# The attentions' output bias, added on GpSimd tile by tile instead of in a run of four

## The chip, the cores and the metric

The kernel runs on one core of one Trainium2 chip. The core has five engines that run side by side, each through its own queue of instructions in a fixed order: TensorE (PE in the profile, with its weight loads as PEld), VectorE (DVE), ScalarE (ACT), GpSimd (POOL) and SyncE (SP, which issues most transfers). They wait for one another by semaphores. The metric is the time of one execution on the device, in microseconds (us).

## The reference, cut to what matters

The input `x` is 2 x 2048 rows of 512 values in f32. Two layers follow each other, each made of a gated cross attention over 128 context rows and a gated feed-forward part:

```python
x = x + tanh(g_xattn[0]) * L0_xattn(layernorm(x), ctx)   # 16 heads of 32
x = x + tanh(g_ffn[0])   * L0_ffn(layernorm(x))          # runs on 256 rows a batch, chosen by a router
x = x + tanh(g_xattn[1]) * L1_xattn(layernorm(x), ctx)   # 16 heads of 64
x = x + tanh(g_ffn[1])   * L1_ffn(layernorm(x))          # 8-bit rows, ternary weights, a conv of 3 taps

def xattn(x, ctx):
    q, k, v = ...                      # projections of x and of the context, by heads
    out = softmax(q @ k.T * scale) @ v
    return out @ Wo + bo
```

The change is about `bo`, the output bias of the two attentions, and about the residual `x` to which the attention's output is added.

## The kernel before, in words

Rows are worked in eight blocks of 512 rows (`BLK`), four tiles of 128 rows each (`TB` = 4). One function, `cross_attention`, serves both attentions. It is unrolled in Python. Its main loop counts units: one unit is one head of one block, so 16 units a block, and a block's later steps are carried out units behind its earlier ones:

- `scores` (L276, PE) and `probabilities` for unit U: the maximum (L119, DVE), the exponentials (L122, ACT), the reciprocal of their sum (L130, DVE), and the multiplication by it (L131, on POOL, 128 x 512 elements).
- `transposed` (L294, PE, copied out by L295) for unit U - 2, and `values` (L302, PE, copied out by L310) for four units together.
- `front` of the next block in unit 10: layer norm with the power `rsqrt` on POOL (L90), the normalisation on DVE (L104), transposes (L113).
- `queries` (L253, PE) of the next four heads.
- `back`, the output projection of the block before. It is a generator of which each unit takes one step, and each step is half a tile: four (first attention) or eight (second) matmuls L320 into a PSUM tile `pp`, a `yield` after the first half and one after the tile. At a tile's end DVE computes `x = pp * gate + x` (L329) and `pp` is free again. PSUM tiles `pp`, `pq` (of `queries`), and those of the feed-forward's matmuls share two buffers in the first attention and three in the second.

The weights' loader multiplies the bias row, spread over all 128 partitions, by the gate once (`load_rest`, L174), so that `back` needs only `x + bo`, on POOL (L316), before L329.

`residual()` gives the four tiles of the residual. In the first attention they lie in SBUF already; in the second they are loaded again from memory.

Beside the first attention runs the router of the first feed-forward, taken step by step by `beside`: statistics (L806, L807), a dot product (L810), and the ranking of rows by comparisons on DVE (L862, L906). Beside the second attention runs the first half of the second feed-forward, by `beside4`: matmuls L1159, then on DVE the scaling (L1169) and two taps of the convolution (L1175), on ACT the middle tap (L1171), and on POOL two small copies that carry the two last columns from block to block (L1168, L1170); later the maxima (L1208 to L1213) and the rounding to integers (L1258, L1264). The second half (L1388) comes last.

A scheduler decides in which order each engine's instructions stand. `keep_in_program_order` pins an instruction behind what has been written before it for the same engine.

Of the kernel before, what the change touches and what calls it, by code (L numbers as in the profile page):

```python
# [22 lines left out]
TB = BLK // P  # L23
# [20 lines left out]
def flamingo_kernel(ctx: ExitStack, tc: tile.TileContext, a: dict, out: bass.AP):  # L44
# [170 lines left out]
    def cross_attention(  # L215
# [96 lines left out]
        def back(n, residual, OT):  # L312

            tiles = residual()
            for t in tiles:
                tc.keep_in_program_order(nc.gpsimd.tensor_tensor(t, t, W.bo, ALU.add))  # L316
            for i, t in enumerate(tiles):
                pp = ps_mm.tile([P, D], F32, name="pp", tag="mm")
                for e in range(nE):
                    nc.tensor.matmul(  # L320
                        pp,
                        OT[e][:, ts(i, P)],
                        W.wo[:, e, :],
                        start=(e == 0),
                        stop=(e == nE - 1),
                    )
                    if e == nE // 2 - 1:
                        yield
                nc.vector.scalar_tensor_tensor(t, pp, W.g, t, ALU.mult, ALU.add)  # L329
                if i == TB - 1:  # L330
                    after_block(n, tiles)
                yield
# [10 lines left out]
        for U in range(N * H + 12):  # L343
            n, u = divmod(U, H)
            if n < N:
                grp, t = divmod(u, 4)
# [18 lines left out]
            if 0 <= V < N * H and V % 4 == 3:  # L365
                n, grp = divmod(V // 4, 4)
                if grp == 0:
                    OT[n] = []
                values(n // NBLK, [AT.pop(i) for i in range(V - 3, V + 1)], OT[n], grp)
                if grp == 3:  # L370
                    out_of = back(n, residual.pop(n), OT.pop(n))
                    if n == N - 1:
                        after_units()
# [1056 lines left out]
    for g in range(LAST + 1):  # L1430
# [5 lines left out]
        for i in range(TB):  # L1436
            t, r, p = ahead.pop(0)
# [78 lines left out]
```

## Time and profile before

| | |
|---|---|
| median of 3 runs | 1788.83 us (1788.56 to 1795.08) |
| the profiled execution | 1791.24 us, of it 1789.2 in the span of the profile |
| PE busy | 1647.3 us, 92% of the span |
| DVE busy | 1250.1 us, 70% |
| ACT busy | 1101.7 us, 62% |
| POOL busy | 536.0 us, 30% |
| bias adds, L316 on POOL | 64 instructions, 1258 ns at the least, 1294 in the middle, 1917 at the most |
| first and last start of L316 | 83.5 us and 1576.1 us |
| first attention and its surroundings, 0 to 560 us | PE busy 498.8, DVE 379.6, POOL 217.1 |
| second attention, 775 to 1620 us | PE busy 805.4, DVE 656.3, POOL 282.1 |
| granted clock of PE | 0.966 of full speed |

In a row of the profile "x64" is the number of instructions, and a line number is the line of the kernel as it was before. In the view of one line the three durations are the shortest, the middle and the longest. In a timeline row the first number is the start and the second the length, both in us from the span's start; neighbouring instructions of one kind are told as one row, with their number. In square brackets stands how long the engine had been idle and what ended the wait. "Excess" in this text is what an instruction takes beyond the time that the same kind with the same shape takes when nothing is in its way.

### The profile page before, as it was taken

The numbers are of one execution on the slowest core, as the hardware profiler recorded it, in microseconds if no ns is written. First come the engines' busy times: TensorE is split into PE (matmuls) and PEld (weight loads), VectorE is DVE, ScalarE is ACT, GpSimd is POOL, SyncE is SP. The second block draws the span as 40 slices with busy tenths as digits, with TensorE's granted clock in tenths as the row PEclk, the third lists the DMA queues.
The fourth block names the chain that finished last, engine by engine and source line by source line (L and its number), as shares of the span: only waits on it lengthen the run. The fifth ranks groups of instructions, "written<-read, shape, count | busy, mean of one in ns | idle before, by whom it ended". The sixth has DMA issues, their size and how long they took to land.

```text
span 1789.2 us, 25277 instructions
## 1 busy us (share of the span) xinstructions
PE 1647.3 (92%) x8122; PEld 864.8 (48%) x8122; DVE 1250.1 (70%) x2544; ACT 1101.7 (62%) x3170; POOL 536.0 (30%) x671
## 2 busy tenths in 40 slices
PE   6999889899999889999999999999999999889968
PEld 3544444455555665755444544445454544434423
DVE  4566878865767443344378789897998789686956
ACT  2876566456553233345367778787787778744555
POOL 2534443342440011033134242432424224231100
PEclk9999999999999999999999999999999999899979
DMA  6011011121007861630012333233242233157374
GB/s 215 7 66 55 35 60 66 59 65 54 25 36 250 287 190 64 190 83 25 19 53 95 127 122 117 91 130 110 94 167 76 87 105 130 62 210 249 123 233 173
DMA packets 119828, 196.99 MB, mean 110 GB/s; under 512 B 12900, under 2 KB 50532, under 8 KB 115984
## 3 DMA queue, kind: packets, MB, share of 16 engines
q1 hardware_dynamic: 117872, 192.23, 31.5%
q0 software_dynamic: 960, 2.10, 0.6%
q8 instruction: 64, 1.05, 0.2%
q10 hardware_dynamic: 864, 1.05, 0.2%
q14 instruction: 68, 0.56, 0.1%
HBM read 120.89 MB, written 74.45 MB: 109 GB/s over the span
## 4 chain that ended last, share of the span: by engine, by line
PE 29%; DVE 15%; DMA 5%; ACT 4%; issue 2%; POOL 1%; SPq 1%; DVEq 0%; POOLq 0%; ACTq 0%
PE pq L253 8%; PE pp L320 8%; DVE h L1175 4%; PE po L302 3%; PE ph L1159 3%; PE sc L276 3%; PE po L1388 2%; PE tp L294 2%; DMA x<-h_d 1%; DVE u L1169 1%; DVE AT L295 1%; DVE nmx L119 1%; DMA hq<-hq_d 1%; DVE hf L1258 1%; DMA h_d<-h 1%
## 5 line engine op out<-in xcount | busy, mean ns | idle before, releaser
L122 ACT ACTIVATE A<-sc,nmx 128x128 f32<-128x128 f32 x1024 | 363.8, 385 | 131.5 <-DVE nmx L119 121.7
L131 POOL TENSOR_TENSOR A<-A,rden 128x512 f32<-128x512 f32 x256 | 275.9, 1079 | 506.7 <-DVE rden L130 410.8
L320 PE MATMUL pp<-L_wo,OT 128*128 128x512 f32 x768 | 366.8, 609 | 18.0 <-DVE x L329 11.9
L253 PE MATMUL pq<-xnT,L_wq 128*128 128x512 f32 x768 | 345.7, 598 | 12.2 <-DVE x L329 12.2
L122 ACT ACTIVATION_READ_ACCUMULATOR A<-sc,nmx 128x1 f32 x1024 | 229.7, 224 | 0.0
L253 PEld LDWEIGHTS pq<-xnT,L_wq 128*128 128x128 f32 x768 | 142.8, 191 | 172.1 <-issue 151.3
L119 DVE TENSOR_REDUCE nmx<-sc 128x4 f32<-128x512 f32 x256 | 168.6, 678 | 71.8 <-PE sc L276 71.6
L320 PEld LDWEIGHTS pp<-L_wo,OT 128*128 128x128 f32 x768 | 136.5, 193 | 164.4 <-issue 133.2
L1175 DVE SCALAR_TENSOR_TENSOR h<-u,cw,h 128x512 f32<-128x512 f32 x256 | 205.0, 834 | 6.0 <-ACT h L1171 5.5
L294 PE MATMUL tp<-ident,A 128*128 128x128 f32 x1024 | 164.4, 284 | 18.7 <-POOL A L131 13.2
L294 PEld LDWEIGHTS tp<-ident,A 128*128 128x128 f32 x1024 | 118.4, 143 | 87.6 <-issue 41.9
L295 DVE COPY AT<-tp 128x512 f32<-128x512 f32 x192 | 129.8, 678 | 43.5 <-PE tp L294 42.8
L276 PEld LDWEIGHTS sc<-L_kT,qT 32*128 32x128 f32 (+1 forms) x2048 | 110.6, 192 | 71.0 <-issue 58.5
L1388 PE MATMUL po<-w2q,hq 128*128 128x512 bf16 x512 | 122.2, 394 | 20.0 <-DVE hq L1370 9.0
L276 PE MATMUL sc<-L_kT,qT 32*128 32x128 f32 (+1 forms) x2048 | 137.0, 293 | 3.8 <-ACT A L122 3.2
L1171 ACT ACTIVATE h<-u,cb,cw 128x512 f32<-128x512 f32 x128 | 99.1, 808 | 64.7 <-DVE u L1169 53.6
L302 PE MATMUL po<-AT,L_v 128*32 128x512 f32 (+1 forms) x512 | 119.3, 657 | 11.7 <-DVE AT L295 11.1
L1159 PE MATMUL ph<-xiT,w1q 128*128 128x512 bf16 x512 | 124.3, 379 | 1.9 <-DVE u L1169 1.5
L1169 DVE TENSOR_TENSOR u<-ph,inv_b 128x512 f32<-128x512 f32 x128 | 84.9, 682 | 31.4 <-PE ph L1159 27.3
L130 DVE RECIPROCAL rden<-den 128x4 f32<-128x4 f32 x256 | 43.3, 169 | 80.0 <-ACT A L122 72.8
L1168 POOL COPY u<-carry 128x2 f32<-128x2 f32 x128 | 48.7, 382 | 167.3 <-DVE h L1175 141.3
L1170 POOL COPY carry<-u 128x2 f32<-128x2 f32 x128 | 49.8, 394 | 150.9 <-DVE u L1169 149.1
(238 smaller groups left out, 2362.6 us busy)
## 6 DMA issues: line engine op xcount, KB each, us to landing
h_d<-h SPq DMA_DIRECT2D x28, 1024.0 KB, 4.1
x_d<-x SPq DMA_DIRECT2D x64, 256.0 KB, 3.1
hf<-h_d SPq DMA_DIRECT2D x64, 256.0 KB, 3.4
x<-x_d SPq DMA_DIRECT2D x61, 256.0 KB, 4.7
x<-h_d SPq DMA_DIRECT2D x48, 256.0 KB, 5.5
x_d<-xo SPq DMA_DIRECT2D x32, 256.0 KB, 2.1
xf<-x_d SPq DMA_DIRECT2D x32, 256.0 KB, 3.6
hq_d<-hi SPq DMA_DIRECT2D x64, 128.0 KB, 1.8
```

The source lines that it names most:

```text
L119: nc.vector.tensor_reduce(nmx, sc, AX.X, ALU.max, negate=True)
L122: nc.scalar.activation(out_tile[:, h, :], sc[:, h, :], AF.Exp, bias=nmx[:, h : h + 1], accum_out=den[:, h : h + 1],)
L131: nc.gpsimd.tensor_tensor(out_tile, out_tile, rden.unsqueeze(2).to_broadcast([P, n, width]), ALU.mult,)
L253: nc.tensor.matmul(pq, W.wq[:, d, ts(e, P)], xnT[:, d, :], start=(d == 0), stop=(d == DC - 1),)
L276: nc.tensor.matmul(sc[h][:, t, :], qT[e % cpg][r, ts(t, P)], W.kT[r, b, e, :], start=True, stop=True,)
L294: nc.tensor.transpose(tp[:, t, :], A[:, t, :], ident)
L295: copy(AT, tp.rearrange("p t n -> p (t n)"))
L302: nc.tensor.matmul(po[h * dh : (h + 1) * dh, :], W.v[:, b, ts(hd, dh)], AT[c * hpc + h], start=True, stop=True,)
L320: nc.tensor.matmul(pp, OT[e][:, ts(i, P)], W.wo[:, e, :], start=(e == 0), stop=(e == nE - 1),)
L1159: nc.tensor.matmul(ph, w1q[:, d, ts(c, P)], xiT[g][:, d, :], start=(d == 0), stop=(d == DC - 1),)
L1175: nc.vector.scalar_tensor_tensor(z, u[:, ds(k, BLK)], cw[:, c, k : k + 1], z, ALU.mult, ALU.add)
L1388: nc.tensor.matmul(po, rows(c), w2q[:, c, :], start=(c == 0), stop=(c == HC - 1))
```

## The change

The four additions of `back` stood in a loop ahead of the first tile's matmuls, so POOL carried them out in a row. They become a function, `add_bias(i)`. It is called for tile 0 at the start, and for tile i + 1 after the `yield` in the middle of tile i. It still pins the addition behind what has been written before it for POOL. The number of additions, their operands and their results stay as they were.

```diff
         def back(n, residual, OT):
 
             tiles = residual()
-            for t in tiles:
+
+            def add_bias(i):
+
+                t = tiles[i]
                 tc.keep_in_program_order(nc.gpsimd.tensor_tensor(t, t, W.bo, ALU.add))
+
+            add_bias(0)
             for i, t in enumerate(tiles):
                 pp = ps_mm.tile([P, D], F32, name="pp", tag="mm")
                 for e in range(nE):
...
                     if e == nE // 2 - 1:
                         yield
+                        if i + 1 < TB:
+                            add_bias(i + 1)
                 nc.vector.scalar_tensor_tensor(t, pp, W.g, t, ALU.mult, ALU.add)
                 if i == TB - 1:
                     after_block(n, tiles)
```

## The prediction

> **What bounds the kernel now.** I read first the page: the profiled execution took 1791.24 us, 2.0 us of it outside the span. Then the line views of the bias add and of what shares time with it, then the timeline around each of the sixteen runs of adds, and last who waits for the step that takes the biased tile.
>
> ```profile
> span 1789.2 us, 25277 instructions
> ...
> PE 1647.3 (92%) x8122; PEld 864.8 (48%) x8122; DVE 1250.1 (70%) x2544; ACT 1101.7 (62%) x3170; POOL 536.0 (30%) x671
> ...
> L131 POOL TENSOR_TENSOR A<-A,rden 128x512 f32<-128x512 f32 x256 | 275.9, 1079 | 506.7 <-DVE rden L130 410.8
> L320 PE MATMUL pp<-L_wo,OT 128*128 128x512 f32 x768 | 366.8, 609 | 18.0 <-DVE x L329 11.9
> L253 PE MATMUL pq<-xnT,L_wq 128*128 128x512 f32 x768 | 345.7, 598 | 12.2 <-DVE x L329 12.2
> ```
>
> TensorE sets the time: 142 us of the span are all that it does not work. POOL, which is all that the change touches, works for 30%. So a POOL edit can only count by what it does to a wait of PE. The last two rows name one: PE stands still for DVE's L329, which adds the scaled output (in PSUM) to the biased tile and so frees the PSUM tile `pp`.
>
> ```profile
> L329 DVE SCALAR_TENSOR_TENSOR x<-pp,gate,x x64: 712/742/752, 86.9 to 1616.8; 128x512 f32<-128x512 f32 x64
> ...
>   PE pq L253: 12.2, 7
>   PE pp L320: 11.9, 5
> ...
>   PE pb L81: 1.2, 1
> ```
>
> These are 13 waits, 25.3 us. By their times in the trace, 12 of them are for the first tile's L329 of a block, the one that follows a run of four bias adds by 2 to 8 us. L329 has its bias add long before. It is late because DVE is late, and the next two views tell why.
>
> ```profile
> L316 POOL TENSOR_TENSOR x<-x,L_bo x64: 1258/1294/1917, 83.5 to 1576.1; 128x512 f32<-128x512 f32 x64
> ```
>
> ```profile
> L1175 DVE SCALAR_TENSOR_TENSOR h<-u,cw,h x256: 714/742/1787, 923.0 to 1686.6; 128x512 f32<-128x512 f32 x128
> ```
>
> ```profile
> 1571.48 6.29 POOL L316 TENSOR_TENSOR x<-x,L_bo 128x512 f32<-128x512 f32 x4
> 1571.55 6.77 DVE L1175 SCALAR_TENSOR_TENSOR h<-u,cw,h 128x512 f32<-128x512 f32 x4 [0.34 <-ACT h L1171]
> ...
> 1578.97 1.24 PE L1159 MATMUL ph<-xiT,w1q 128*128 128x512 bf16 x5 [1.20 <-DVE u L1169]
> ```
>
> ```profile
> 1370.35 5.85 POOL L316 TENSOR_TENSOR x<-x,L_bo 128x512 f32<-128x512 f32 x4
> ...
> 1372.46 4.95 DVE L1175 SCALAR_TENSOR_TENSOR h<-u,cw,h 128x512 f32<-128x512 f32 x4
> ...
> 1378.03 0.71 DVE L329 SCALAR_TENSOR_TENSOR x<-pp,gate,x 128x512 f32<-128x512 f32 x1
> ...
> 1378.80 2.41 PE L253 MATMUL pq<-xnT,L_wq 128*128 128x512 f32 x5 [1.82 <-DVE x L329]
> ```
>
> Four L1175 alone are 4 x 0.74 = 2.97 us. Beside the run at 1571.5 they take 6.77, and the four adds 6.29 where alone they take 4 x 1.26. One by one in that run DVE's take 1.73, 1.76, 1.75, 1.75 us and POOL's 1.26, 1.73, 1.71, 1.72: the two go in lockstep, each held until the other is through. The same happens to L906 (median 0.34, up to 1.38 us), L862, L104 and L1258, all of which read SBUF alone; L119, L295, L1169 and L329, which read PSUM, keep their times beside an add.
>
> **The change part by part.** It removes and adds no arithmetic. In the built program the orders of PE, DVE, ACT and SP are what they were, DMA issues included; on POOL the adds of tiles 1 to 3 of each block move back, mostly to just behind a later L131, in the very last block to behind carry copies (L1168, L1170). In the last block of the first attention three stay in a row, so 46 of the 64 move.
>
> *Relief.* I measured, for each run of adds, by how much the DVE instructions in it exceed the untouched time of their own shape (L1175 0.74, L1258 0.66, L906 0.34, L104 0.52, L862 0.28 to 0.66 by width): 34.9 us over the sixteen runs. Of that 10.9 belongs to instructions begun by the end of the first add, which stays. Of the rest only as much counts as PE then waited. Run start: excess left, PE's wait behind it, the smaller of the two: 135.7: 1.32, 2.25, 1.32. 189.2: 2.03, 5.99, 2.03. 253.4: 1.32, 3.03, 1.32. 309.8: 2.02, 0.26, 0.26. 464.5: 1.02, 1.46, 1.02. 940.3: 1.79, 1.76, 1.76. 1049.7: 2.12, 1.85, 1.85. 1155.8: 2.07, 2.01, 2.01. 1261.4: 1.64, 1.22, 1.22. 1370.4: 2.24, 1.82, 1.82. 1477.7: 2.14, 2.31, 2.14. 1571.5: 3.06, 1.20 (for L1169), 1.20. The four other runs (83.5, 378.3, 525.3, 845.4) had no such excess or no wait behind it: 0. Sum: 5.95 in the first attention, 12.00 in the second, 17.95 us.
>
> Here a rule can be weighed. The row: an L1175 that starts 0.07 us behind an add ends 1.73 us later, an excess of 1.0. The Trainium skill, page "SBUF — State Buffer", section "Who interferes with whom", says that DVE with two SBUF inputs and a GpSimd instruction that reads SBUF exclude each other for the whole of an instruction, the first to start winning. By that the L1175 would take 1.19 + 0.74 = 1.93, an excess of 1.19, and with all excesses 1.19 times as large, capped by the same PE waits, the relief would be about 19.2. I take the row: 17.95.
>
> *The same collisions elsewhere.* A moved add can hold a DVE instruction at its new place. No row shows that place; the nearest is L131, the same kind of POOL instruction, strewn just so: its 256 instructions (median 1.04 us) cost DVE 43.1 us of excess, 0.168 each. By length, x 1.27/1.04, 0.206 for an add, x 46 = 9.5 us of DVE. What of that PE feels lies between 0 (the L329 of tiles 1 to 3 come 4 to 23 us apart, and PE waited only once, 0.41 us, for one of these) and all. I take half, since in the runs so much reached PE only where L329 was next: 4.7, with 0 and 9.5 kept as ends.
>
> *POOL's queue.* Behind a moved add stand L131, the small carry copies (L1168, L1170) and the power for the layer norm (L90), each at most 1.3 us later. For L131: near the runs, the transposes that read it come 1.2 to 20 us after it, and it no longer queues behind a run (at 83.5 it was 2.0 us late); 0. Carry copies: the run held them by up to 6 us, now one add does; 0, or a gain of a few tenths. L90: DVE's normalisation waits for it, and in two blocks (189.2 and 253.4) an add now stands ahead of it. In the first the next transposes of probabilities start 5 us after their operands; in the second PE waited at 271.55 for DVE already, so one add counts: 1.3 (ends 0 and 1.9, the longest add). The adds themselves: placed in this trace, tile 1's still ends 3 us or more ahead of its L329. The residual tiles are loaded as before, and no add waited for one: 0.
>
> *Waits.* DVE gets 12 more semaphore instructions (L329 waits for its own add), 21 ns each by the wait rows of that line: 0.25.
>
> Sum: -17.95 + 4.7 + 1.3 + 0.25 = -11.7 us against the profiled execution's 1791.24. That one is 2.4 above the median of the runs, and I carry the difference to the median: 1788.83 - 11.7 = 1777.1. With the ends: -17.95 + 0.25 = -17.7 (1771.1), and -17.95 + 9.5 + 1.9 + 0.25 = -6.3 (1782.5). About 0.5% (8.9 us) is what a measurement of this kernel can tell from no change.
>
> **The rivals.** *Hidden after all.* PE at 92% has waits one behind the other: if what L329 gives up is taken by the next wait (for `AT`, for `xi`, for the probabilities), little is left. For it: at 309.8 a DVE excess of 2.0 stood before a PE wait of only 0.26. Against: after its wait behind the runs of the second attention PE goes through 5 us and more of queued matmuls without another. Keeping a quarter of the relief: -4.5 + 1.3 + 0.25, and some collisions cancel it: 1788.8, within 4 either way.
>
> *Slower: the strewn adds meet more DVE work than the runs did.* A run in lockstep holds each DVE instruction once per add; a single add put where DVE is in a row of L1175 does the same, and 46 of them move. At 1.0 us each and the share that reached PE in the runs (17.95 of 22.8 us, 79%), it turns into a loss when 17.95 / (46 x 0.79) = 49% of the moved adds hold one. L131 does so in 68 of 256 cases, 27%, which speaks against it. At 80%: 46 x 0.8 x 0.79 = 29.1, less 17.95, plus 1.55: +12.7, 1801.5.
>
> *The change does not do what it says.* Out by the built order but for one block: no change, 1788.8.
>
> **How the numbers follow.** Forecast (1771 to 1783) 70%, of which 58 of 100 in all lie beyond 8.9 us; hidden 20%; strewn collisions 8%, of which 6 beyond +0.5%; not done 2%. Faster 0.58, same 0.36, slower 0.06. The range for 8 in 10 takes the forecast's ends and the hidden case up to a little above no change: 1770 to 1790.
>
> **What would show it.** Right: the adds no longer come as rows of four, and beside those of tiles 1 to 3 fewer are held beyond 1.5 us; PE's waits for L329 fall from 25.3 us to under 12; L1175's and L906's busy sums fall by several us. The step on strewn collisions is wrong if DVE's excess beside the adds is as large as before (34.9 us). The prediction fails if PE's waits for L329 shrink and the span does not (hidden), or if new PE waits for `AT` or L1169 stand behind the places of the moved adds (slower).

## The result, and the profile after

The changed kernel takes 1775.11 us (median of 6 runs, 1772.26 to 1777.77) against 1788.69 for the kernel before, run beside it (6 runs, 1785.28 to 1795.08). The ratio is 0.9919, 95% interval 0.9899 to 0.9938: 13.6 us faster. The forecast was -11.7 us, to 1777.1. The profiled execution of after took 1774.49 us.

Line numbers move down: the add L316 is L319 in after, L320 is L325, L329 is L336, L1175 is L1182, L1169 is L1176, L906 is L913. In the experiments they move by their own few lines; the text uses the numbers of before where no fence is quoted.

The page of after:

```profile
span 1772.0 us, 25243 instructions
...
PE 1640.7 (93%) x8076; PEld 864.2 (49%) x8122; DVE 1237.6 (70%) x2544; ACT 1102.7 (62%) x3170; POOL 536.8 (30%) x671
...
L131 POOL TENSOR_TENSOR A<-A,rden 128x512 f32<-128x512 f32 x256 | 281.1, 1100 | 494.6 <-DVE rden L130 400.5
L325 PE MATMUL pp<-L_wo,OT 128*128 128x512 f32 x768 | 366.1, 608 | 12.1 <-DVE u L1176 6.4
L253 PE MATMUL pq<-xnT,L_wq 128*128 128x512 f32 x768 | 344.9, 596 | 1.4 <-DVE x L336 1.2
```

POOL is as busy as before (536.8 us, 536.0 before) and DVE executes the same 2544 instructions, but DVE is busy 12.5 us less (1250.1 before). That is about as much as the time fell, though the experiments will show that the two do not always go together. The projection and `queries` rows show where PE got its share: the idle time ahead of `queries` fell from 12.2 to 1.4 us, and of L325's 12.1 us 6.4 are now a wait for the scaling and 5.7 one for the biased tile (11.9 before). PE is 6.6 us less busy. 4.2 us of that stand in two groups of which the trace of after has fewer records: the feed-forward's L1159, 512 rows before and 477 after (124.3 and 122.2 us), and L1388, 512 and 501 (122.2 and 120.1). The rest may go with PE's granted clock, 0.969 after and 0.966 before.

The three line views that were shown of before:

```profile
L336 DVE SCALAR_TENSOR_TENSOR x<-pp,gate,x x64: 711/741/753, 85.0 to 1600.8; 128x512 f32<-128x512 f32 x64
...
  PE pp L325: 5.7, 3
...
  PE pq L253: 1.2, 2
```

```profile
L319 POOL TENSOR_TENSOR x<-x,L_bo x64: 1263/1274/1721, 81.6 to 1591.3; 128x512 f32<-128x512 f32 x64
```

```profile
L1182 DVE SCALAR_TENSOR_TENSOR h<-u,cw,h x256: 714/743/1757, 917.4 to 1671.2; 128x512 f32<-128x512 f32 x128
```

PE's waits for L329 fell from 25.3 us in 13 to 6.9 in 5. Single instructions are as fast as before at the shortest and in the middle, and a collision still costs about as much when it happens (the longest L1182 takes 1757 ns, 1787 before; the longest add 1721 ns, 1917 before). There are fewer: 8 of the 64 adds now take more than 1.5 us, 16 before.

The timeline at the last block, whose run of four at 1571.5 was shown of before:

```profile
1556.03 1.27 POOL L319 TENSOR_TENSOR x<-x,L_bo 128x512 f32<-128x512 f32 x1
1556.11 3.73 DVE L1182 SCALAR_TENSOR_TENSOR h<-u,cw,h 128x512 f32<-128x512 f32 x4 [0.34 <-ACT h L1178]
...
1559.76 1.28 DVE L1176 TENSOR_TENSOR u<-ph,inv_b 128x512 f32<-128x512 f32 x2
...
1561.31 1.27 POOL L319 TENSOR_TENSOR x<-x,L_bo 128x512 f32<-128x512 f32 x1
...
1562.43 0.75 DVE L336 SCALAR_TENSOR_TENSOR x<-pp,gate,x 128x512 f32<-128x512 f32 x1 [1.40 <-PE pp L325]
```

The first add still meets the four L1182 that it met before. It holds one of them: the four take 3.73 us, where a row of four with no add beside it takes 2.73 here (1363.45 in the next fence) and the run of four adds made it 6.77. The second add comes 5 us later, when the two L1176 are through, and falls into the 1.40 us in which DVE waits for PE.

The timeline at the block whose run stood at 1370.4:

```profile
1361.34 1.28 POOL L319 TENSOR_TENSOR x<-x,L_bo 128x512 f32<-128x512 f32 x1
1363.45 2.73 DVE L1182 SCALAR_TENSOR_TENSOR h<-u,cw,h 128x512 f32<-128x512 f32 x4
...
1366.91 0.74 DVE L336 SCALAR_TENSOR_TENSOR x<-pp,gate,x 128x512 f32<-128x512 f32 x1
...
1367.80 1.46 PE L253 MATMUL pq<-xnT,L_wq 128*128 128x512 f32 x3
```

Here one add is through before the row of L1182 begins, L336 is early, and PE's `queries`, which waited 1.82 us in before, carry no wait.

### The profile page after: what moved, and what is told of

It is laid out like the page before. It is cut to its first block, busy times and chain, and to the rows that moved or that the text cites. A ratio compares the mean times of both kernels' runs of the same rounds, so it can differ in the third digit from the quotient of the medians.

```text
span 1772.0 us, 25243 instructions
## 1 busy us (share of the span) xinstructions
PE 1640.7 (93%) x8076; PEld 864.2 (49%) x8122; DVE 1237.6 (70%) x2544; ACT 1102.7 (62%) x3170; POOL 536.8 (30%) x671
## 4 chain that ended last, share of the span: by engine, by line
PE 50%; DVE 25%; ACT 9%; DMA 9%; issue 3%; POOL 3%; SPq 1%; ACTq 0%; DVEq 0%; POOLq 0%
PE pp L325 12%; PE pq L253 10%; PE po L302 4%; PE tp L294 4%; DVE h L1182 4%; PE sc L276 4%; ACT A L122 3%; PE ph L1166 3%; DVE nmx L119 2%; DVE marks L869 2%; PE po L1395 2%; PE pu L655 2%; PE acc L640 2%; PE pw L655 2%; DMA h_d<-h 1%
## 5 line engine op out<-in xcount | busy, mean ns | idle before, releaser
L131 POOL TENSOR_TENSOR A<-A,rden 128x512 f32<-128x512 f32 x256 | 281.1, 1100 | 494.6 <-DVE rden L130 400.5
L325 PE MATMUL pp<-L_wo,OT 128*128 128x512 f32 x768 | 366.1, 608 | 12.1 <-DVE u L1176 6.4
L325 PEld LDWEIGHTS pp<-L_wo,OT 128*128 128x128 f32 x768 | 136.3, 193 | 157.5 <-issue 132.5
L1182 DVE SCALAR_TENSOR_TENSOR h<-u,cw,h 128x512 f32<-128x512 f32 x256 | 196.1, 800 | 5.9 <-ACT h L1178 5.4
L295 DVE COPY AT<-tp 128x512 f32<-128x512 f32 x192 | 129.8, 678 | 40.7 <-PE tp L294 40.1
L1395 PE MATMUL po<-w2q,hq 128*128 128x512 bf16 x501 | 120.1, 391 | 20.9 <-ACT hq L1375 9.2
L302 PE MATMUL po<-AT,L_v 128*32 128x512 f32 (+1 forms) x512 | 116.8, 642 | 11.9 <-DVE AT L295 11.4
L1166 PE MATMUL ph<-xiT,w1q 128*128 128x512 bf16 x477 | 122.2, 379 | 2.6 <-DVE u L1176 0.5
L1176 DVE TENSOR_TENSOR u<-ph,inv_b 128x512 f32<-128x512 f32 x128 | 84.9, 682 | 30.5 <-PE ph L1166 26.5
L1175 POOL COPY u<-carry 128x2 f32<-128x2 f32 x128 | 49.5, 389 | 172.5 <-DVE h L1182 149.4
L1177 POOL COPY carry<-u 128x2 f32<-128x2 f32 x128 | 50.9, 404 | 141.7 <-DVE u L1176 140.6
```

The costliest lines, as they stand in the source:

```text
L131: nc.gpsimd.tensor_tensor(out_tile, out_tile, rden.unsqueeze(2).to_broadcast([P, n, width]), ALU.mult,)
L295: copy(AT, tp.rearrange("p t n -> p (t n)"))
L302: nc.tensor.matmul(po[h * dh : (h + 1) * dh, :], W.v[:, b, ts(hd, dh)], AT[c * hpc + h], start=True, stop=True,)
L325: nc.tensor.matmul(pp, OT[e][:, ts(i, P)], W.wo[:, e, :], start=(e == 0), stop=(e == nE - 1),)
L1166: nc.tensor.matmul(ph, w1q[:, d, ts(c, P)], xiT[g][:, d, :], start=(d == 0), stop=(d == DC - 1),)
L1182: nc.vector.scalar_tensor_tensor(z, u[:, ds(k, BLK)], cw[:, c, k : k + 1], z, ALU.mult, ALU.add)
```

## The experiments

Two theories were to be told apart, with parts of each. The *held access*: an add that reads SBUF and a DVE instruction that fetches operands through SBUF alone hold each other, a run of four does so up to four times in a row just ahead of a first tile's L329, and PE pays. *POOL's queue*: four adds occupy POOL for 5 to 6 us, and what stands behind them comes late. A third possibility was that L329 waits for its own add.

The table gives each kernel's median, its ratio to the kernel before with the 95% interval, the difference of the medians of one comparison, the DVE busy time of its page less the 1250.1 us of before, and, worked out from the traces, DVE's excess beside the adds and PE's waits for L329. Excess is what an instruction takes above the lower quartile of its own line and shape, where that is over 0.1 us; it is put to the POOL instruction that overlaps it most. By this count before has 30.9 us beside the adds and 46.6 beside L131, and PE waits 25.4 us for L329. (The 34.9 of the prediction took all DVE instructions of the sixteen stretches. Some expectations below give 17.9 for after in place of 20.6: that figure is 2.7 us short, as much as one held instruction of L441 and two of L1220 make in after. Another 2.3 us of after stand beside the carry copies that follow an add.)

| kernel | time, us | ratio (95%) | difference | DVE busy, less before's | beside adds | PE for L329 |
|---|---|---|---|---|---|---|
| after | 1775.11 | 0.9919 (0.9899-0.9938) | -13.6 | -12.5 | 20.6 | 6.9 |
| e1 no adds | 1758.75 | 0.9825 (0.9805-0.9845) | -31.0 | -31.6 | 0 | 4.1 |
| e2 fills in the run's place | 1760.09 | 0.9830 (0.9809-0.9852) | -29.7 | -29.4 | 2.7 | 5.4 |
| e3 idle run, one tile | 1773.90 | 0.9916 (0.9897-0.9935) | -15.8 | -10.9 | 20.3 | 17.5 |
| e9 idle run, two tiles | 1786.83 | 0.9976 (0.9963-0.9989) | -3.9 | +0.2 | 30.3 | 25.3 |
| e13 run of eight | 1828.68 | 1.0203 (1.0167-1.0239) | +36.8 | +25.7 | 54.6 | 32.5 |
| e11 first tiles' adds alone | 1765.28 | 0.9855 (0.9829-0.9881) | -26.6 | -26.2 | 6.3 | 6.8 |
| e12 moved adds alone | 1765.44 | 0.9857 (0.9832-0.9883) | -26.4 | -17.9 | 13.0 | 3.4 |
| e4 change in first attention | 1785.27 | 0.9971 (0.9960-0.9982) | -4.5 | -7.4 | 26.4 | 17.7 |
| e5 change in second attention | 1779.78 | 0.9933 (0.9912-0.9954) | -11.0 | -5.3 | 24.5 | 12.6 |
| e7 first add a unit earlier | 1774.26 | 0.9907 (0.9883-0.9931) | -16.5 | -11.2 | 21.2 | 5.7 |
| e10 strewn transfers | 1768.15 | 0.9855 (0.9833-0.9877) | -22.6 | -24.5 | 0.3 | 4.3 |
| e14 a run of transfers | 1780.92 | 0.9938 (0.9915-0.9962) | -11.0 | -32.0 | 0.1 | 5.7 |

**What do the adds cost, and through what?** First they were left out.

```diff
-            for t in tiles:
-                tc.keep_in_program_order(nc.gpsimd.tensor_tensor(t, t, W.bo, ALU.add))
```

> The 64 bias adds are left out (the output lacks bo), all else stands as before. Theory (DVE's instructions and the adds hold each other, DVE comes late to L329, PE waits): with no adds all 31 us of DVE excess beside them go, also that beside the first add of each block, so this is the floor of what any placing of the adds can reach. PE's waits for L329 fall from 25.4 us to 6 or less, the time to 1767 to 1774, a little below the changed kernel. Rival (queue: what stood behind the run on POOL came late): the same size, so this run tells only how much is to be had. Rival (chance of the start and of transfers): 1780 or more.

Measured: 1758.75 us, 8 us below the range that was expected. Its page:

```profile
span 1751.6 us, 25162 instructions
...
PE 1630.8 (93%) x8076; PEld 859.2 (49%) x8122; DVE 1218.5 (70%) x2544; ACT 1101.7 (63%) x3170; POOL 441.7 (25%) x607
```

The 64 adds take 90 us of an engine that is idle for 70% of the time, and cost the kernel 31 us. DVE does the same 2544 instructions in 31.6 us less. So the change recovers somewhat under half of what the run cost.

In e2 the run's place is filled with POOL instructions that only write, about as long in all:

```diff
-            for t in tiles:
-                tc.keep_in_program_order(nc.gpsimd.tensor_tensor(t, t, W.bo, ALU.add))
+            for _ in tiles:
+                for k in (D, D, P):
+                    tc.keep_in_program_order(nc.gpsimd.memset(W.bo[:, 0:k], 0.0))
```

> Each of the four adds of a run is replaced, in its place, by three fills of the bias tile (512, 512 and 128 columns, about 1.2 us together), which write SBUF and read nothing; the output lacks bo. POOL is occupied as long as before and what stands behind the run waits as long. Theory of the held access: L1175, L1258 and L906 (two inputs in SBUF) are no longer held, their excess beside the run goes to near 0; L862 and L104 (one input in SBUF) may still be. PE's waits for L329 in the second attention (10.97 us in six waits) go to 2 or less, the time falls to 1773 to 1780. Rival (POOL's queue): POOL is as late as before, so the time stays at 1786 to 1791.

The view of the fills:

```profile
L317 POOL MEMSET L_bo<- x192: 199/524/1401, 83.2 to 1553.6; 128x512 f32 x128, 128x128 f32 x64
```

They sum to 85.6 us, as much as the 85.6 us of the adds in after, and the time, 1760.09 us, is that of e1 within 1.3 us; 1773 to 1780 had been expected. L1175, L1258 and L906, with two inputs in SBUF, have no excess left. The 2.7 us that stay are on L862, L104 and L1264, with one. POOL's queue behind a run therefore costs next to nothing, and nearly all of the run's 31 us goes when nothing reads SBUF there beside DVE. (L329's wait for its own add goes with it; e9 below bounds that.)

e3 and e9 keep a run of reading instructions, but of work that nobody waits for; the bias is not added to the rows.

```diff
-            for t in tiles:
-                tc.keep_in_program_order(nc.gpsimd.tensor_tensor(t, t, W.bo, ALU.add))
+            for _ in tiles:
+                # e3: tensor_tensor(W.bo, W.bo, W.bo, ALU.subtract)
+                # e9: tensor_tensor(W.bo, W.bo, W.wo[:, 0, :], ALU.subtract)
```

> The run of four stays, as the same instruction with the same size, but on the bias tile alone (a subtraction of it from itself), so no residual tile and no L329 waits for it; the output lacks bo. Theory of the held access: the same excess on DVE (30 us) and the same waits of PE for L329 (24 to 26 us), time 1786 to 1791, as before. Rival (L329 waits for its own add, by the data or the semaphore): with that gone the time falls to 1775 to 1780.

e3 missed its expectation (1773.90 us, where even the rival had said 1775 to 1780), and its view says why it was not the test that it was meant to be:

```profile
L316 POOL TENSOR_TENSOR L_bo<-L_bo x64: 1032/1040/1568, 83.7 to 1562.7; 128x512 f32<-128x512 f32 x64
```

With one tile as both operands the instruction takes 1040 ns, not 1274, and the longest 1568. The run is shorter and holds DVE for 20.3 us, not 30.9. e9 takes two tiles:

> As the run of four on the bias tile alone, but the second operand is another tile (rows of the output weights), so that each instruction again reads two tiles and takes 1.26 us; in the run before, both operands were one tile, each instruction took 1.04 us, and DVE's excess beside them was 20.3 us in place of 30.9. No L329 waits for it; the output lacks bo. Held access: DVE's excess beside the run is 29 to 32 us again and the time 1785 to 1792. Rival (L329's own wait for the add is what costs): excess as large, but the time stays at 1772 to 1779. In between (1779 to 1785): both have a part.

Its view of the run, then its timeline where the four L1175 are L1177, then who waited for L329 (L331 here):

```profile
L317 POOL TENSOR_TENSOR L_bo<-L_bo,L_wo x64: 1262/1277/1799, 82.5 to 1571.0; 128x512 f32<-128x512 f32 x64
```

```profile
1566.34 6.30 POOL L317 TENSOR_TENSOR L_bo<-L_bo,L_wo 128x512 f32<-128x512 f32 x4
1566.41 6.77 DVE L1177 SCALAR_TENSOR_TENSOR h<-u,cw,h 128x512 f32<-128x512 f32 x4 [0.34 <-ACT h L1173]
```

```profile
L331 DVE SCALAR_TENSOR_TENSOR x<-pp,gate,x x64: 715/742/753, 85.9 to 1611.4; 128x512 f32<-128x512 f32 x64
...
  PE pq L253: 12.6, 7
  PE pp L322: 11.2, 5
...
  PE pb L81: 1.5, 1
```

The 6.30 and 6.77 us, and the 25.3 us in 13 waits, are those of before, though L331 needs nothing from this run. So PE does not wait for L329 because L329 waits for its add. What may remain of a wait for the own add is the 3.9 us by which e9 is faster (2.0 to 6.6 by the interval), and whether it is that or something else in which e9 differs was not separated.

In e13 the run is doubled: each tile has the bias added, taken off again, and so ends without it.

```diff
             for t in tiles:
-                tc.keep_in_program_order(nc.gpsimd.tensor_tensor(t, t, W.bo, ALU.add))
+                for op in (ALU.add, ALU.subtract):
+                    tc.keep_in_program_order(nc.gpsimd.tensor_tensor(t, t, W.bo, op))
```

> The run has eight instructions in place of four: each tile's add and, behind it, a subtraction that takes it off again (the output lacks bo). Held access, one for one: the run lasts 5 to 7 us longer and meets more DVE work; DVE's excess beside it grows from 31 to between 45 and 60 us, the time by 14 to 30, to 1804 to 1820. Rival (PE's waits absorb it, or POOL's length alone counts): the same DVE excess, or a time within 6 us of before.

```profile
PE 1660.7 (91%) x8076; PEld 869.5 (48%) x8122; DVE 1275.8 (70%) x2544; ACT 1103.3 (60%) x3170; POOL 632.8 (35%) x735
...
L317 POOL TENSOR_TENSOR x<-x,L_bo 128x512 f32<-128x512 f32 x128 | 181.7, 1434 | 3.9
```

The lines are the page's. DVE's excess rises by 23.7 us, as the theory has it, but the time rises by 36.8, above what was expected. In PE's waits the largest addition is 8.5 us for L131 (21.7 against 13.2), which now stands behind eight adds; those for L329 grow by 7.1. A queue that cost nothing behind four adds seems to cost something behind eight. The granted clock was 0.961 against 0.966; what that makes of the rest is told under the clock below.

**The parts of the change.** e11 keeps the first tile's add and leaves those of tiles 1 to 3 out; e12 keeps these where the change puts them and leaves the first out.

```diff
# e11, against after
                     if e == nE // 2 - 1:
                         yield
-                        if i + 1 < TB:
-                            add_bias(i + 1)
# e12, against after
-            add_bias(0)
```

> Only the first tile's add of each block is left, where it stands in both kernels; tiles 1 to 3 lack bo. This measures the prediction's first term by itself: what the run's other three adds cost. By its list: 17.95 us less than before (1790 - 18 = 1772), if only what PE waited for L329 or L1169 counts. If the time follows DVE's excess one for one: excess beside adds about 9 us in place of 31, so 20 to 24 us less, 1766 to 1770.

> As the changed kernel, with the first tile's add left out: only the 48 adds of tiles 1 to 3, at their new places. Against the kernel with no adds (1758.8) this measures the cost of the moved adds: by the prediction 4.7 (0 to 9.5) for collisions, 1.3 for the power behind an add and 0.25 for waits: 1765, with ends 1759 to 1770. One for one with DVE's excess: of the 17.9 us that the changed kernel has beside adds, 7 to 10 lie at the moved ones: 1766 to 1769.

The views of the adds in e11 and in e12:

```profile
L319 POOL TENSOR_TENSOR x<-x,L_bo x16: 1261/1276/1642, 82.5 to 1550.3; 128x512 f32<-128x512 f32 x16
```

```profile
L319 POOL TENSOR_TENSOR x<-x,L_bo x48: 1262/1272/1718, 87.1 to 1587.3; 128x512 f32<-128x512 f32 x48
```

Taking three adds of each run away gains 26.6 us (21.3 to 30.6), to 1765.28, just below both of the figures expected; e12's 1765.44 is what the prediction's terms had given. The 48 strewn adds hold DVE in 16 places, 33% of them, for 13.0 us, and by themselves cost 4.6 us more than no adds at all (the difference of -26.4 and -31.0; 6.7 between the medians themselves). Put back beside the first adds they cost 13.0 (-13.6 less -26.6; 9.8 between the medians). DVE's excess adds up (6.3 + 13.0 = 19.3, and 20.6 in after); its effect on the time does not quite, though with intervals of 4 us on each side that is no more than suggested.

e4 and e5 make the change in one attention only and keep the run in the other (`bias` is true in the first).

```diff
+            spread = bias            # e4; in e5: not bias
+            for i in range(1 if spread else TB):
+                add_bias(i)
...
                         yield
+                        if spread and i + 1 < TB:
+                            add_bias(i + 1)
```

> The adds are strewn in the first attention alone; in the second they stay in runs. By the prediction's sum: relief 5.95 us, less half of the collisions at the new places (22 x 0.2 / 2 = 2.2) and 1.3 for the layer norm's power: -2.4, 1786.3; with the ends 1783 to 1789. PE's waits for L329 in the second attention stay at 11 us in six waits, those in the first fall from 14.4 to about 7. A rival in which the gain lies in the first attention (whose runs held more DVE work): 1778 or less.

> The adds are strewn in the second attention alone; in the first they stay in runs. If the time follows DVE's excess beside POOL one for one, as the runs so far suggest (all strewn: 12.6 us less excess, 13.6 us less time; strewn in the first alone: 5.7 and 4.5; adds left out: 30.4 and 31.0), the excess beside the second attention's adds falls from 17.0 to 9.5 us and the time by 7 to 10, to 1779 to 1783, and the two halves add up to the whole. By the prediction's sum: relief 12.0, less half of 24 x 0.206: -9.5. Rival (only the waits for L329 count): 11 us of waits go but for 0.2, so -11 or more.

They gain 4.5 and 11.0 us, together 15.5 where the whole gains 13.6. The second attention, where rows of L1175 stand ahead of L329, brings about two thirds, as the prediction's list of waits had it (5.95 and 12.00). e5 does not follow DVE's excess one for one: DVE is busy 5.3 us less and its excess falls by 6.4, the time by 11.0. PE's waits for L329 fall by 12.8, and the rival that counted these alone had said -11 or more.

**PE's waits and PE's clock.** The two theories leave something out. In the profile's records PE's granted clock has two values, full and half; 0.966 is their mean over the span. Before has 18 stretches at half clock, the longest of 13.7 us, 123 us in all. In the 3.4 us ahead of each of them PE worked for 65% or less. One of them begins at 198.1 us, in PE's longest wait for L329, and the matmul behind that wait takes 1.22 us; L320 takes 592 ns in the middle.

```profile
200.03 1.22 PE L320 MATMUL pp<-L_wo,OT 128*128 128x512 f32 x1 [5.99 <-DVE x L329]
```

So PE can gain or lose in two ways, by its waits and by what it works at half clock. The table gives both for some of the profiled executions. The last column is an estimate: half of PE's busy time within the stretches at half clock.

| kernel | span, us | PE's waits | lost at half clock |
|---|---|---|---|
| before | 1789.2 | 135.5 | 48.8 |
| after | 1772.0 | 122.5 | 44.1 |
| e1 | 1751.6 | 112.0 | 36.0 |
| e3 | 1772.7 | 126.5 | 40.7 |
| e9 | 1782.9 | 133.1 | 44.7 |
| e11 | 1765.6 | 117.2 | 45.8 |
| e12 | 1766.6 | 120.2 | 42.0 |
| e13 | 1827.4 | 158.4 | 62.2 |

In all thirteen kernels the two columns together make up the change of the span against before within 3 us. This closes most of what e13 left open: its span is 38.2 us longer, 22.9 of it waits and 13.4 half clock. It has 26 stretches at half clock, and six of them begin in a wait for L329 of 2.9 to 5.3 us or at most 1.2 us behind it; in before one does, in e1 none.

What sets the clock is not shown. It differs between executions of one kernel too: in the 59 of before that ran beside the experiments it lies between 0.963 and 0.973, and the time is about 1.2 us longer for each 0.001 less. By this estimate 2 to 7 us of some differences in the first table go with the clock: before has 0.967 in the middle, after and e11 have 0.969, e1 0.970, e3 and e12 0.972, e13 0.961. PE's waits do not depend on that estimate, and by them the parts of the change are: the three adds left out of the run -18.3 us (before to e11), the same three put in at their new places +5.3 (e11 to after) or +8.2 (e1 to e12).

**Can more be had?** In e7 the first add, too, leaves its place: the rows are asked for and the first add is done one unit before `back` starts. The rest is as in after.

```diff
+            if 0 <= V < N * H and V % H == H - 1 - EARLIER:      # EARLIER = 1
+                rows[V // H] = residual.pop(V // H)()
+                add_bias(rows[V // H][0])
```

> As the changed kernel, and the first tile's add of each block too is moved, one unit earlier. The changed kernel's excess beside adds (17.9 us) is for a good part at the first adds, in the first attention above all (its waits for L329 that remain, 6.7 us, stand right behind them). Held access: if the new place meets less DVE work, the excess falls to 10 to 15 us and the time to 1768 to 1773; if it meets as much, 1773 to 1778. Rival (what is left at L329 is the wait for the first add itself): the same gain whatever DVE's excess does, 1768 to 1770.

It came out as after does (1774.26): the new place meets as much DVE work (21.2 us of excess, 20.6 in after). Moving an add is worth only what the new place lacks.

e10 is e7 with the additions done by transfers that accumulate, issued by POOL. It does all of the work.

```diff
-            tc.keep_in_program_order(nc.gpsimd.tensor_tensor(t, t, W.bo, ALU.add))
+            tc.keep_in_program_order(nc.gpsimd.dma_start(out=t, in_=W.bo, accum_op=ALU.add))
```

> The adds are strewn with the first one unit earlier, and carried out by transfers that add the bias tile onto the residual tile, issued by POOL, in place of POOL's instruction: POOL reads no SBUF for them. Held access: DVE's excess beside adds nearly goes, as with the adds left out, and the time falls to 1757 to 1766 if the transfers land before L329 (5 us and more are there for them). Rivals: transfers land late, and L329 and PE wait for them (1775 and more); or the issue of a transfer occupies POOL as long and is held by DVE's instructions as well (1768 to 1775).

The view of the bias tile, and the engines on the page:

```profile
L313 POOL DMA_DIRECT2D x<-L_bo x64: 856/876/1531, 80.3 to 1589.2; - x64
...
DMA to landing us min/median/max: 3.2/3.5/9.6
```

```profile
PE 1642.2 (93%) x8122; PEld 863.4 (49%) x8122; DVE 1225.6 (69%) x2544; ACT 1102.5 (62%) x3170; POOL 503.5 (28%) x671
```

1768.15 us, 22.6 faster than before, and the fastest kernel here that does all of the work. DVE's excess beside the issues is 0.3 us. About 7 us of it returned beside L131 (53.8 us, 46.6 before), which falls on other DVE instructions now. The time is 2 us above what was expected of free access, and in the range of the rival in which the issues hold DVE; the 0.3 us speak against that rival. PE's waits are 120.5 us, 8.5 more than with no adds at all.

e14 makes the same transfers in the run's place, four at a time, which tells whether the strewing is still needed:

> The run of four stays in its place, carried out by transfers that add the bias tile, issued by POOL one behind the other (876 ns each when strewn). POOL reads no SBUF, so DVE is not held: as with the strewn transfers (1768), if four transfers at once land before L329, which comes 2 to 8 us behind the run: 1764 to 1771. If they land later than that, PE waits for L329 in blocks where it follows by 2 to 3 us: up to 2 us a block, 1770 to 1795. If the order of the adds mattered by itself, whatever carries them out, this would be 10 us and more slower than the strewn transfers.

1780.92 us, though its DVE is the least busy of all that add the bias (1218.1 us). By the differences that is 11.6 us slower than the strewn transfers, as the last of the expected cases had it, and not for the reason that the second gave: PE waits only 5.7 us for L329. Its waits, and then those of e10 (us in total, times, longest):

```profile
DVE hf L1258 <- DMA hf<-h_d: 27.1, 22, 2.4
...
PE po L302 <- DVE AT L295: 20.9, 15, 4.2
```

```profile
DVE hf L1264 <- DMA hf<-h_d: 19.7, 21, 2.2
...
PE po L302 <- DVE AT L295: 11.3, 15, 1.4
```

And two places of its timeline:

```profile
1165.08 0.69 DVE L1258 TENSOR_TENSOR hf<-hf,s_b 128x512 f32<-128x512 f32 x1 [1.91 <-DMA hf<-h_d]
...
1171.36 1.12 PE L302 MATMUL po<-AT,L_v 128*64 128x512 f32 x2 [4.16 <-DVE AT L295]
```

```profile
1559.53 3.58 POOL L316 DMA_DIRECT2D x<-L_bo  x4 [0.34 <-issue]
...
1568.04 0.75 DVE L329 SCALAR_TENSOR_TENSOR x<-pp,gate,x 128x512 f32<-128x512 f32 x1 [4.84 <-DMA x<-L_bo]
...
1568.85 1.55 PE L320 MATMUL pp<-L_wo,OT 128*128 128x512 f32 x3 [1.68 <-DVE x L329]
```

The loss is in the second attention: at the `scores` of the last block's first head e14 is 11 us ahead of e10 in the first attention (429.9 and 441.0) and 3 us behind it in the second (1437.7 and 1434.6), 9 us at the end of the last L329 (1609.1 and 1599.9). DVE waits 7.4 us longer for loads of the feed-forward's rows (`hf`), and in the first of these places the copy L295 that PE needs stands behind such a wait; once a biased tile itself is late by 4.84 us. A transfer takes 5.8 us to land in a run and 3.5 when strewn, by the median; the loads of `hf` take 3.4 in both. That a burst of four transfers delays single loads fits the rows, but no run isolates it. The mixture that these two runs point to (a run of transfers in the first attention, strewn ones in the second) was not tried.

## Why the prediction was right, point by point

- **The mechanism.** Right. Reading adds hold DVE (30.9 us of excess beside the adds of before, 2.7 beside the fills of e2), the first tile's L329 is late without waiting for its add (e9), and PE's waits for L329 fell to 6.9 us, under the 12 that were given as the sign. L1175's busy sum fell by 8.9 us (205.0 to 196.1), L906's by 5.0 (20.4 to 15.4).
- **The relief, -17.95.** As a count of PE's waits it was right: with the run's other three adds left out (e11) those for L329 fall by 18.6 us, all of PE's waits by 18.3. As a change of the time it was too small: -26.6, 21.3 to 30.6. The term that the sum lacks is PE's clock, which it put at nothing without saying so: of e11's 23.6 us shorter span 18.3 are waits and about 3 half clock. What is left of the 26.6, some 5 us, is open. The 19.2 that the prediction worked out from the Trainium skill's "fully blocks" is as near to 18.6 as the 17.95 taken from the row, so the waits do not decide between them.
- **The collisions elsewhere, +4.7 (half of 9.5).** DVE's share was set too low: 13.0 us in e12, in 33% of the adds, against 9.5 and L131's 27%. What of it reaches PE was about as assumed: with the 1.3 for L90 the sum has 6.0 us, and PE's waits grow by 5.3 (e11 to after) or 8.2 (e1 to e12). The time grows by 4.6 when the moved adds stand alone and by 13.0 beside the first adds.
- **The sum.** In PE's waits -18.3 + 5.3 = -13.0 stands against -17.95 + 4.7 + 1.55 = -11.7. In time -26.6 + 13.0 = -13.6: both terms are some 7 to 9 us too small there, and that they offset each other was luck. Of the 17.2 us by which the profiled executions differ, 13.0 are waits and about 4.7 half clock, which the forecast did not have. DVE's excess fell by 10.3 us (30.9 to 20.6) and its busy time by 12.5.
- **POOL's queue, 0 and 1.3 for L90.** e2 shows that POOL's occupancy costs 1.3 us by the medians (e1 to e2), which is within their intervals. For the normalisation, the waits of after have

```profile
DVE xn L104 <- POOL L_ln_rstd L90: 8.2, 6, 2.4
```

  which was 6.0 us in 6 before: 2.2 us of DVE, of which no run shows how much PE felt.
- **DVE's waits, 0.25.** 46 semaphore instructions on L329 instead of 34, as counted.
- **Hidden after all.** In part it happened: PE's waits for L329 fell by 18.5 us, its other waits rose by 5.5 (110.1 to 115.6). Their sum fell by 13.0. Collisions at the new places would look the same, so the two are not told apart. The rival's quarter would have kept 4.5 us of relief.
- **Slower by more collisions.** The share of held adds was 33%, below the 49% at which it would have lost.

## What to carry to other kernels

A GpSimd instruction that reads SBUF is not free because GpSimd is idle: look at what DVE does in the same microseconds, and compare the longest time of a DVE line with its median. Where DVE feeds an engine that is over 90% busy, count that engine's waits and what it works at half clock; here the two made up every change within 3 us. DVE's own loss is a rougher guide: with the adds left out the time fell by as much (31.0 and 31.6 us), in one attention alone by 0.6 times (4.5 and 7.4) and by twice as much (11.0 and 5.3). An instruction that is to be moved is best placed where DVE waits or reads PSUM. A transfer that accumulates avoided the collision (0.3 us of excess), though four in a row gained 11.0 us here where strewn ones gained 22.6.

## What the runs showed that was not expected

- A POOL subtraction of a 128 x 512 f32 tile with one tile as both operands took 1.04 us, with two tiles 1.26 (e3 and e9).
- POOL fills of the same tile (0.52 us for 512 columns) beside the same DVE rows left 2.7 us of excess in 192 instructions. The Trainium skill, page "SBUF — State Buffer", section "Who interferes with whom", says that a DVE instruction with two SBUF inputs contends with a GpSimd instruction that reads SBUF and not with one that only writes it; e2 agrees.
- 64 POOL adds of 1.26 us cost this kernel 31 us, 0.48 each. As a run they hold DVE for 0.48 us each (30.9 / 64), strewn for 0.27 (13.0 / 48).
- In e13 the time grew by 36.8 us where DVE's excess grew by 23.7; in e3 it shrank by 15.8 where the excess shrank by 10.6. PE's time at half clock moved along in both, by 13.4 and by 8.1 us, and e9's 3.9 us are of that size too (4.1).
